# Moving one group of TensorE transposes ahead of a matmul in an attention step

## The chip, the cores and the metric

The kernel runs on one NeuronCore of a Trainium2 chip. The metric is device time in microseconds. Five runs of the kernel before took 1192.12, 1193.80, 1199.54, 1202.81 and 1203.57 us; the median is 1199.54 us. One further run was made with the hardware profiler on; all views of the trace quoted here come from that one.

## The reference

The input x holds 64 sequences of 64 tokens with 512 features, in fp32. Four layers are added to it, each with its own residual, and each takes an index per sequence:

```python
x = x + L0(x, cond)            # per sequence a 64 x 64 matrix out of 200, over the tokens
x = x + L1(x, adapter1)        # 512 x 512 product plus a low-rank adapter, rank 16 of 4
x = x + L2(x, tables, kv_lens) # attention with a paged cache, a window of 256 positions
x = x + L3(x, adapter3)        # 512 x 512 product plus a low-rank adapter, rank 16 of 8
```

The change lies in the attention. For each sequence, 8 query heads share 4 key heads (64 features each). The new keys (normed and rotated) and new values of the 64 tokens are written into blocks of the cache. A token attends to the 256 positions up to its own: `softmax(q @ k.T / 16)` over them, times the values. The cache is reached through a table of blocks, 16 positions a block, of which at most 21 bear on a sequence.

## The kernel before, in words

There are two stages. In the first one (0 to about 460 us) the layers 0 and 1 and the key and value projections run over 32 tiles of 128 tokens. In the second one (from about 476 us on) the attention and layer 3 run, and the change touches that stage alone.

The order of the instructions is written out by hand (`tc.manual_schedule()`): what the program issues first on an engine runs first on it. The framework only adds the waits between engines.

The second stage is a loop over 128 **steps**. A step is one sequence `b` and one pair `gp` of key heads; `q = b // 4` is the **group** of four sequences, so a group has 8 steps, and `i = s % 8` is the **position** of a step in its group. Every step `s` does this, in this order on TensorE:

- `scores(s + 1)` (L983): the products of queries and turned keys of the next step, into the banks `psc` of PSUM;
- `turn_p(s)` (L1025): six transposes of the softmax weights, into the banks `pp`;
- for positions 4 to 7 `k_turn(q + 1, *turn1)`, the **first key turn**;
- one part of layer 3 of the group before (`out_product` L1059, `ranks` L1067, `y_first` L1078, `y_rest` L1084 and L1086), or in the first two groups a query projection (L263);
- `values(s)` (L1041): the turned weights times the values, into the one bank of `psO`;
- for positions 3 to 6 `k_turn(q + 1, *turn2)`, the **second key turn**.

Then the next step's `scores` follow. A key turn (`k_turn`, L175) makes four transposes of 84 x 128 pieces of the next group's keys out of the tile `k` (named `k2` in the code) into the only bank of the pool `psK`, and two copies (L183, L184) take them from there to `kT_mem`, on ScalarE where `o4` is even and on VectorE where it is odd. The eight turns of a group are spread like this:

```python
turns = {3: (None, (0, 0)), 4: ((1, 0), (0, 1)), 5: ((1, 1), (0, 2)), 6: ((1, 2), (0, 3)),
         7: ((1, 3), None)}
```

The pairs are `(gp, o4)`. So the second turn at position 3 is the first of its group, and the one at position 6, `(0, 3)`, is the last for the key heads `gp = 0`; the step at position 7 begins with `scores(s + 1)`, which is the first to read them.

What else bears on the turns: the tile `k` is filled by gathers (`k_load`), copies (`k_copy`, L157) and last by `k_patch(q + 1)` at position 1, an indirect DMA from GpSimd's queue that writes the rows of new keys over the old ones. On VectorE a step has `maxima` (L999), a copy of one turned half (L1032), `shares` (L1016, L1017) and, where `gp` is 1, the middle part of `window` (L972). On ScalarE it has the other copy of L1032, `exponentials` (L1009), the outer parts of `window` (L971, L973), the copy `keep_o` of the values' product (L1049, after the second turn's copies) and, where `gp` is 0, `v_copy` (L197), for which a `v_patch` on GpSimd's queue waits. The last group has no next one, so 15 groups have key turns inside the loop.

Of the kernel before, what the change touches and what calls it, by code (L numbers as in the profile page):

```python
# [50 lines left out]
def kernel(  # L51
# [89 lines left out]
    def bank(pool, name):  # L141
        return pool.tile([P, 512], F32, name=name, tag="b")
# [5 lines left out]
    def k_load(q, h):  # L148

        if q < B // 4:  # L150
            gather(kt[:NP, 2 * h : 2 * h + 2].rearrange("p g o d -> p (g o d)"), k_halves,
                   ik_old[:, h, q : q + 1])
# [8 lines left out]
    def k_patch(q):  # L161

        if q < B // 4:
            gather(k2[:NP].rearrange("p o g d -> p (o g d)"), pk, ik_new[:, q : q + 1], NWR - 1)

    def kT(q, gp):
        return kT_mem[q % 2][:, gp].rearrange("p (b o c i) -> p b o c i", b=4, o=3, c=4)

    def k_turn(q, gp, o4, pool=psK):

        if q >= B // 4:
            return
        ps = bank(pool, f"psk{q}_{gp}_{o4}")[:, : 4 * NP].rearrange("p (o r) -> p o r", o=4)
        for oq in range(4):
            PE.transpose(ps[:, oq, :],  # L175
                         k2[:NP, 4 * oq + o4, 2 * gp : 2 * gp + 2].rearrange("p g d -> p (g d)"),
                         ident[:NP, :NP])
        if o4 < 3:
            dst = kT(q, gp)[:, :, o4, :3]
        else:  # L180
            dst = kT(q, gp)[:, :, :, 3]
        copy = V.tensor_copy if o4 % 2 else S.copy
        copy(dst[:, :, :, :NR], ps[:, :3].rearrange("p c (b j) -> p b c j", b=4))  # L183
        copy(dst[:, :, :, NR:], ps[:, 3].rearrange("p (b c j) -> p b c j", b=4, c=3))  # L184

    def v_load(b):
        if b < B:
            for g in range(NG):
                gather(vs_mem[:NV, b % 2, g].rearrange("p o d -> p (o d)"), v_rows,
                       iv_old[:, b, g : g + 1])  # L190

    def vt(b):
        return vt_mem[:, b % 4].rearrange("p (o g d) -> p o g d", g=NG, d=HD)
# [5 lines left out]
    def v_patch(b):  # L199
        if b < B:  # L200
            gather(vt_mem[:NV, b % 4], pv.rearrange("w (q r) -> (w q) r", q=4),
                   iv_new[:, b : b + 1], NWR * 4 - 1)

    def v_share(b):

        if b < B:
            for c in range(3):
                DMA.dma_start(out=vt(b)[96:NVK, c], in_=vt(b)[32 * c : 32 * c + 28, 3])
# [49 lines left out]
    def product_q(n, pool):  # L258
        if 0 <= n < NTILE:
            psq[n] = bank(pool, f"q{n}")  # L260
            xt = x2s.pop(n)
            for c in range(KC):
                PE.matmul(psq[n], lhsT=xt[:, c, :], rhs=wq_sb[:, c, :],  # L263
                          start=(c == 0), stop=(c == KC - 1))

    def norm_q(n):

        if not 0 <= n < NTILE:
            return lambda: None
        rest = turned(n, psq.pop(n), NH, qsc, "q", qp1, qp2)  # L270

        def second():
            qheads[n] = rest()
        return second

    def turn_q(n, pool):
        if not 0 <= n < NTILE:
            return
        ps = bank(pool, f"pst{n}").rearrange("p (gp h b t) -> p gp h b t", gp=2, h=2, b=2)
        hq = qheads.pop(n).rearrange("p (gp h g) d -> p gp h (g d)", gp=2, h=2)  # L280
        for gp in range(2):
            for h in range(2):
                PE.transpose(ps[:, gp, h].rearrange("p b t -> p (b t)"), hq[:, gp, h], ident)
        qt = qp2.tile([P, 2, 2, 2, T], F32, name=f"qt{n}", tag="qt")
        for gp in range(2):
            S.copy(qt[:, gp].rearrange("p b h t -> p h b t"), ps[:, gp])
        lo = n % 2 * 2
        for gp in range(2):
            S.dma_start(out=qd[:, n // 2, gp, lo : lo + 2], in_=qt[:, gp])
# [668 lines left out]
    def q_load(q):  # L958
        if q < B // 4:
            qts[q] = ap2.tile([P, 2, 4, 2, T], F32, name=f"qs{q}", tag="qs")  # L960
            DMA.dma_start(out=qts[q], in_=qd[:, q])

    def x_load(q):
        xqs[q] = ap2.tile([P, KC, 256], F32, name=f"xq{q}", tag="xq")
        DMA.dma_start(out=xqs[q], in_=x2d[:, :, q * 256 : (q + 1) * 256])
# [9 lines left out]
    def scores(s):  # L975

        if s >= NST:
            return
        q, b, gp = steps[s]
        pscs[s] = [bank(psC, f"psc{s}_{g}")[:, :NS] for g in range(2)]  # L980
        for g in range(2):
            gs = slice(g * HD, (g + 1) * HD)
            PE.matmul(pscs[s][g], lhsT=qts[q][gs, gp, b % 4].rearrange("p h t -> p (h t)"),  # L983
                      rhs=kT(q, gp)[gs, b % 4].rearrange("p o c i -> p (o c i)"),
                      start=True, stop=True)
# [4 lines left out]
    def maxima(s):  # L990

        if s >= NST:
            return
        b = steps[s][1]
        sms[s] = []
        for g in range(2):
            sm = sm_mem[:, (2 * s + g) % 4]
            mn = ap4.tile([P, 1], F32, name=f"mn{s}_{g}", tag="mn")
            V.tensor_tensor_reduce(rows4(sm)[:, :, :, :28], rows4(pscs[s][g]), rows4(pens[b]),  # L999
                                   SCALE, 3.0e38, ALU.add, ALU.min, mn)  # L1000
            rsum = ap4.tile([P, 1], F32, name=f"rsum{s}_{g}", tag="rsum")
            sms[s].append((sm, mn, rsum))

    def exponentials(s):
        if s >= NST:
            return
        for sm, mn, rsum in sms[s]:
            w = rows4(sm)[:, :, :, :28]
            S.activation(w, w, AF.Exp, bias=mn, scale=-1.0, accum_out=rsum)  # L1009
# [9 lines left out]
    def turn_p(s):  # L1019

        pps[s] = []
        for g in range(2):
            pp = bank(psP, f"pp{s}_{g}")[:, : 3 * P].rearrange("p (o r) -> p o r", o=3)
            for o in range(3):
                PE.transpose(pp[:NVK, o, :], sms[s][g][0][:, o * P : o * P + NVK], ident)  # L1025
            pps[s].append(pp)

    def keep_p(s):
        pTs[s] = []
        for g in range(2):  # L1030
            pT = ap2.tile([NVK, 3, P], F32, name=f"pT{s}_{g}", tag="pT")
            (V.tensor_copy if g else S.copy)(pT, pps[s][g][:NVK])  # L1032
            pTs[s].append(pT)

    def values(s):

        q, b, gp = steps[s]
        po = bank(psO, f"po{s}")[:, :P]
        for o in range(3):
            for g in range(2):  # L1040
                PE.matmul(po[g * HD : (g + 1) * HD, :], lhsT=vt(b)[:NVK, o, 2 * gp + g],  # L1041
                          rhs=pTs[s][g][:, o, :], start=(o == 0), stop=(o == 2))
        return po

    def keep_o(s, po):
        q, b, gp = steps[s]
        if s % 8 == 0:
            oTs[q] = ap2.tile([P, 2, 4, 2, T], F32, name=f"oT{q}", tag="oT")
        S.copy(oTs[q][:, gp, b % 4].rearrange("p h t -> p (h t)"), po)  # L1049
# [67 lines left out]
    for s, (q, b, gp) in enumerate(steps):  # L1117
        i = s % 8
        turn1, turn2 = turns.get(i, (None, None))
        if i == 0 and q:  # L1120
            x_load(q)
        if i == 2:
            q_load(q + 1)
        if gp == 0:
            v_load(b + 3)
        else:
            v_share(b + 1)
            v_patch(b + 2)
        if i == 1:
            k_patch(q + 1)  # L1130
        if i in (2, 3):
            k_load(q + 2, i - 2)
        scores(s + 1)
        turn_p(s)
        if 0 < s < 16:
            turn_q(nq + s - 2, psO)
        if turn1:
            k_turn(q + 1, *turn1)
        maxima(s + 1)
        keep_p(s)  # L1140
        exponentials(s + 1)
        second = norm_q(nq + s if q < 2 else -1)
        if parts:
            parts.pop(0)()
        if q < 2:
            product_q(nq + s + 1, psM)
            x2_load(nq + s + 3)
        shares(s + 1)
        second()
        if gp:  # L1150
            window(b + 2)
        po = values(s)
        if turn2:
            k_turn(q + 1, *turn2)
        keep_o(s, po)
        if gp == 0:
            v_copy(b + 2)
        if i == 0:
            k_copy(q + 1, 3)
        elif i > 4:  # L1160
            k_copy(q + 2, i - 5)
        if i == 7:
            parts += last_parts(q)
# [53 lines left out]
```

## Time and profile before

| | |
|---|---|
| median of five runs | 1199.54 us |
| the profiled run, its own time | 1194.86 us |
| its span, first to last instruction | 1193.1 us |
| TensorE matmuls busy | 1097.9 us (92%) |
| VectorE, ScalarE, GpSimd busy | 752.8, 570.8, 615.2 us |
| 700 to 800 us: TensorE, VectorE, ScalarE, GpSimd busy | 95.76, 64.56, 62.50, 63.76 us of 100 |

PE is the matmul part of TensorE, PEld its weight loads, DVE is VectorE, ACT ScalarE, POOL GpSimd, SP the engine that only issues DMAs. A line of a timeline has the start in us, the length in us, engine, line of the code, operation, what is written and read, and in square brackets the time that the engine sat idle before it with what ended the idle time. The fp32 matmuls run as two passes each, so six products of `values` show as x12; the transposes show as x1 each.

### The profile page before, as it was taken

To read this page: it belongs to the slowest core of one execution; us is meant where nothing else is said; L and a number is where in the kernel's file an instruction comes from. 1 tells how busy PE (TensorE), PEld (TensorE's weight loads), DVE (VectorE), ACT (ScalarE), POOL (GpSimd) and SP (SyncE) were. 2 spreads that over 40 slices of the span, in tenths; PEclk is the share of its full clock that TensorE was granted. 3 is DMA by queue.
4 is the path that set the end of the run, shared out by engine and by line. 5 is a ranking of instruction groups with operands and counts; after the bars stand their busy time and mean duration, and the time that the engine had idled before them with its cause. 6 is when DMAs were issued, how large, how long until landed. Compare 5 with 4: busy or idle time off the path is not lost.

```text
span 1193.1 us, 17686 instructions
## 1 busy us (share of the span) xinstructions
PE 1097.9 (92%) x5622; PEld 638.1 (53%) x5622; DVE 752.8 (63%) x2313; ACT 570.8 (48%) x1472; POOL 615.2 (52%) x601
## 2 busy tenths in 40 slices
PE   4998899999899995897999999999999999999998
PEld 4444444444444443455566556656656665665665
DVE  3676445756666593786667666666766676666561
ACT  1332212223224332555566666656666665666561
POOL 3153231333263253588766667667666666756620
PEclk9999999999899997898999999999999999999999
DMA  7266622132433264354565566557556755755420
GB/s 260 108 256 227 228 91 91 61 125 73 156 100 98 85 173 130 105 146 127 133 160 147 141 138 159 133 131 170 144 138 152 168 133 136 164 146 138 99 66 36
DMA packets 129820, 163.20 MB, mean 137 GB/s; under 512 B 58079, under 2 KB 96891, under 8 KB 125545
## 3 DMA queue, kind: packets, MB, share of 16 engines
q0 software_dynamic: 63872, 85.04, 29.3%
q1 hardware_dynamic: 46416, 53.89, 14.9%
q10 hardware_dynamic: 19440, 23.15, 5.7%
q8 instruction: 45, 0.74, 0.3%
q14 instruction: 47, 0.39, 0.1%
HBM read 139.66 MB, written 50.33 MB: 159 GB/s over the span
## 4 chain that ended last, share of the span: by engine, by line
PE 63%; DVE 10%; DMA 9%; ACT 6%; issue 5%; POOL 2%; ACTq 1%; POOLq 0%; DVEq 0%; SPq 0%
PE pso L1059 7%; PE pp L1025 6%; PE po L1041 6%; PE psc L983 6%; PE q L263 6%; PE ps L787 5%; PE kv L820 5%; PE psy L1084 5%; PE psy L1078 5%; DMA k<-pk,ik_new 4%; PE psk L175 3%; PE psxa L1067 2%; PE psy L1086 2%; PE ps L789 2%; PE psz L772 1%
## 5 line engine op out<-in xcount | busy, mean ns | idle before, releaser
L65 POOL DMA_INDIRECT vs_mem<-in_vblk_dram,iv_old x256 | 310.7, 1214 | 77.4 <-issue 65.8
L1009 ACT ACTIVATE sm_mem<-sm_mem,mn 128x336 f32<-128x336 f32 x256 | 145.6, 574 | 32.9 <-DVE mn L999 31.8
L65 POOL DMA_INDIRECT vt_mem<-pv,iv_new x64 | 79.7, 1245 | 130.1 <-ACT vt_mem L197 68.7
L999 DVE CUSTOM_DVE_ANT_0 sm_mem<-psc,pen 128x336 f32<-128x336 f32 x256 | 118.7, 500 | 14.1 <-PE psc L983 12.4
L1041 PEld LDWEIGHTS po<-pT,vt_mem 124*64 124x64 f32 x1536 | 83.2, 137 | 75.1 <-ACT sm_mem L1009 53.1
L1059 PE MATMUL pso<-oT,woT_sb 128*128 128x256 f32 x512 | 123.3, 385 | 0.0
L263 PE MATMUL q<-wq_sb,x2q 128*128 128x512 f32 x256 | 120.5, 616 | 0.0
L983 PE MATMUL psc<-kT_mem,qs 64*128 64x336 f32 x512 | 108.1, 497 | 10.8 <-DVE kT_mem L184 10.8
L1041 PE MATMUL po<-pT,vt_mem 124*64 124x128 f32 x1536 | 114.4, 282 | 3.6 <-ACT pT L1032 3.6
L787 PE MATMUL ps<-kT_mem,kT_mem 128*128 128x512 f32 x256 | 116.9, 600 | 0.6 <-PE ps_fill L493 0.6
L1017 DVE TENSOR_SCALAR sm_mem<-sm_mem,rsum 128x336 f32<-128x336 f32 x256 | 110.8, 433 | 9.1
L820 PE MATMUL kv<-wkv_sb,xr 128*128 128x512 f32 x256 | 115.4, 595 | 0.4 <-ACT va L828 0.4
L1025 PE MATMUL pp<-ident,sm_mem 128*124 128x128 f32 x768 | 113.5, 282 | 2.5 <-DVE sm_mem L1017 1.8
L1025 PEld LDWEIGHTS pp<-ident,sm_mem 128*124 128x124 f32 x768 | 81.1, 139 | 63.6 <-issue 51.5
L248 POOL TENSOR_TENSOR q<-q,rsq 128x512 f32<-128x512 f32 x30 | 32.1, 1074 | 141.1 <-DVE rsq L246 110.4
L1059 PEld LDWEIGHTS pso<-oT,woT_sb 128*128 128x128 f32 x512 | 92.7, 193 | 12.4 <-ACT oT L1049 2.7
L787 PEld LDWEIGHTS ps<-kT_mem,kT_mem 128*128 128x128 f32 x256 | 49.2, 193 | 61.3 <-issue 60.1
L263 PEld LDWEIGHTS q<-wq_sb,x2q 128*128 128x128 f32 x256 | 49.9, 200 | 59.2 <-issue 58.9
L175 PE MATMUL psk<-ident,k 84*128 84x84 f32 x512 | 63.4, 250 | 16.4 <-ACT kT_mem L184 13.7
L820 PEld LDWEIGHTS kv<-wkv_sb,xr 128*128 128x128 f32 x256 | 47.0, 191 | 57.1 <-issue 55.6
L1032 ACT COPY pT<-pp 124x384 f32<-124x384 f32 x128 | 61.7, 482 | 31.3 <-PE pp L1025 25.2
L973 ACT ACTIVATE pen<-pen,edge 128x336 f32<-128x336 f32 x64 | 36.9, 576 | 79.8 <-DVE pen L972 79.8
(223 smaller groups left out, 1783.5 us busy)
## 6 DMA issues: line engine op xcount, KB each, us to landing
xt<-in_x_dram SPq DMA_DIRECT2D x32, 256.0 KB
x2d<-xr SPq DMA_DIRECT2D x8, 1024.0 KB
x2q<-x2d SPq DMA_DIRECT2D x32, 256.0 KB
qd<-qt ACTq DMA_DIRECT2D x64, 128.0 KB
qs<-qd SPq DMA_DIRECT2D x16, 512.0 KB
xq<-x2d SPq DMA_DIRECT2D x16, 512.0 KB
out_dram<-ys ACTq DMA_DIRECT2D x32, 256.0 KB
vt_mem<-vt_mem SPq DMA_DIRECT2D x192, 28.0 KB
```

Source lines behind the costliest of these rows:

```text
L65: G.indirect_dma_start(out=dst, out_offset=None, in_=src, in_offset=bass.IndirectOffsetOnAxis(ap=idx, axis=0), **more,)
L175: PE.transpose(ps[:, oq, :], k2[:NP, 4 * oq + o4, 2 * gp : 2 * gp + 2].rearrange("p g d -> p (g d)"), ident[:NP, :NP])
L263: PE.matmul(psq[n], lhsT=xt[:, c, :], rhs=wq_sb[:, c, :], start=(c == 0), stop=(c == KC - 1))
L787: PE.matmul(ps, lhsT=wb_sb[:, c, oc * P : (oc + 1) * P], rhs=x1_mem[:, c, :], start=(c == 0), stop=False)
L820: PE.matmul(pskv[n], lhsT=xrs[s][:, c, i * P : (i + 1) * P], rhs=wkv_sb[:, c, :], start=(c == 0), stop=(c == KC - 1))
L983: PE.matmul(pscs[s][g], lhsT=qts[q][gs, gp, b % 4].rearrange("p h t -> p (h t)"), rhs=kT(q, gp)[gs, b % 4].rearrange("p o c i -> p (o c i) ...
L999: V.tensor_tensor_reduce(rows4(sm)[:, :, :, :28], rows4(pscs[s][g]), rows4(pens[b]), SCALE, 3.0e38, ALU.add, ALU.min, mn)
L1009: S.activation(w, w, AF.Exp, bias=mn, scale=-1.0, accum_out=rsum)
L1017: V.tensor_scalar(w, w, rsum, None, ALU.mult)
L1025: PE.transpose(pp[:NVK, o, :], sms[s][g][0][:, o * P : o * P + NVK], ident)
L1041: PE.matmul(po[g * HD : (g + 1) * HD, :], lhsT=vt(b)[:NVK, o, 2 * gp + g], rhs=pTs[s][g][:, o, :], start=(o == 0), stop=(o == 2))
L1059: PE.matmul(o, lhsT=woT_sb[:, c, ec * P : (ec + 1) * P], rhs=oT[:, c // 2, :, c % 2, :], start=(c == 0), stop=(c == 3))
```

## The change

The second key turn is issued ahead of `values(s)` in place of after it. Nothing else moves; the copies of the turn still stand ahead of `keep_o` on ScalarE, and in the same place among the others on VectorE.

```diff
         if gp:
             window(b + 2)
-        po = values(s)
         if turn2:
             k_turn(q + 1, *turn2)
+        po = values(s)
         keep_o(s, po)
```

## The prediction

> **What bounds the kernel now.** I read the page's busy shares first, then TensorE's waits over the loop, then the timeline around each second key turn. TensorE is busy for 92% of the span and nearly 97% in a full group of the loop (40.38 of the 41.80 us from 812.00 to 853.80), while no other engine passes 28 us there. So a move inside TensorE's queue is worth what it does to TensorE's few waits. These are they, from 470 to 1160 us (who waited for what: total us, times, longest us):
>
> ```profile
> PE psk L175 <- ACT kT_mem L184: 13.7, 24, 4.0
> PE psc L983 <- DVE kT_mem L184: 10.8, 16, 1.2
> ...
> PE psk L175 <- DMA k<-pk,ik_new: 2.8, 5, 0.8
> ```
>
> Three of them touch the moved turns. The second line is the scores of position 7, which need keys whose turn TensorE issued just before: 14 times 0.66 us (9.3 us) and once 1.17 us. The third is the turn of position 3, which waits for the patch of the keys to land. The first is the first turn of positions 4 and 6, which wait for ScalarE to empty the one bank of `psK`; 4.0 us of its 13.7 lie ahead of the loop.
>
> The other work in the queue is only put in another order: four transposes take 0.44 us from start to the next group's start (838.99 to 839.43), the values' 12 passes 0.81 us (838.18 to 838.99). The change moves 15 x 4 = 60 turns, no copy and no DMA; VectorE's, ScalarE's, GpSimd's and SP's queues keep their order.
>
> **Position 6, the wait that should go.** TensorE first, then VectorE, same microseconds:
>
> ```profile
> 838.18 0.88 PE L1041 MATMUL po<-pT,vt_mem 124*64 124x128 f32 x12
> 838.99 0.51 PE L175 MATMUL psk<-ident,k 84*128 84x84 f32 x4
> 840.16 0.84 PE L983 MATMUL psc<-kT_mem,qs 64*128 64x336 f32 x4 [0.66 <-DVE kT_mem L184]
> ```
>
> ```profile
> 838.76 0.39 DVE L1017 TENSOR_SCALAR sm_mem<-sm_mem,rsum 128x336 f32<-128x336 f32 x1
> 839.54 0.42 DVE L183 COPY kT_mem<-psk 128x252 f32<-128x252 f32 x1 [0.38 <-PE psk L175]
> 839.88 0.23 DVE L184 COPY kT_mem<-psk 128x84 f32<-128x84 f32 x1
> ```
>
> After the move the transposes start at 838.18 and end by 838.69. One would write off the whole wait, but VectorE is not free then: the shares stand ahead of the copies in its queue and end at 839.15. So the copy starts near 839.12 (such neighbours overlap by some hundredths) in place of 839.54, and the scores, which come 0.62 us after the copy's start, at 839.74 in place of 840.16. **Gain 0.42 us**, and a wait of about 0.3 us is left, since TensorE has done turn and values by 839.43. All 14 groups from the second on show the same 0.66 us: 14 x 0.42 = 5.9 us. In the first group VectorE is busy with the queries' norms up to the very copy:
>
> ```profile
> 539.73 0.67 DVE L244 TENSOR_TENSOR q<-q,mq 128x512 f32<-128x512 f32 x1
> 540.33 0.41 DVE L183 COPY kT_mem<-psk 128x252 f32<-128x252 f32 x1
> ```
>
> There the turn ended at 539.77 and the copy waited for VectorE alone, so its 1.17 us stay: gain 0. The bounds of this gain are 0 (all groups like the first) and the whole 10.5 us (9.3 + 1.17).
>
> **Position 3, the wait that should grow.** The turn of position 3 needs the patch, which lands near the values:
>
> ```profile
> 694.79 0.88 PE L1041 MATMUL po<-pT,vt_mem 124*64 124x128 f32 x12
> 696.50 0.51 PE L175 MATMUL psk<-ident,k 84*128 84x84 f32 x4 [0.83 <-DMA k<-pk,ik_new]
> 696.94 0.84 PE L983 MATMUL psc<-kT_mem,qs 64*128 64x336 f32 x4
> ```
>
> ```profile
> 852.89 9.73 DMA k<-pk,ik_new
> 862.62 0.04 issue
> 862.67 0.51 PE psk L175 x4
> ```
>
> Today 0.81 us of values run while the patch is still under way. With the turn ahead, they wait behind it. From the trace's semaphore records I took the landing (the last of the patch's sixteen updates, plus the 0.04 us of the row above) against the start of the values, group by group, in us: -3.24, -0.70, -0.28, 0.62, 1.71, 0.53, 0.75, 0.18, 1.46, 1.14, -0.15, -0.03, 0.57, 1.58, 1.24. A negative one costs nothing. Where it is over 0.81 TensorE waits already (5 groups, the 2.8 us above) and will wait 0.81 longer: **5 x 0.81 = 4.05 us**. The five between 0 and 0.81 are new waits, but part of each is time that the first turn of position 4 loses today anyhow, as ScalarE comes to the copy only behind the window:
>
> ```profile
> 821.99 0.58 ACT L973 ACTIVATE pen<-pen,edge 128x336 f32<-128x336 f32 x1 [2.00 <-DVE pen L972]
> 822.48 0.36 ACT L183 COPY kT_mem<-psk 128x252 f32<-128x252 f32 x1
> ```
>
> ```profile
> 823.01 0.51 PE L175 MATMUL psk<-ident,k 84*128 84x84 f32 x4 [0.30 <-ACT kT_mem L184]
> ```
>
> That copy's time is set by VectorE's part of the window, not by TensorE's turn, so a later turn eats that wait first: 0.62 - 0.30, 0.53 - 0.30, 0.75 - 0.61, nothing of 0.18, 0.57 - 0.24, in all 1.0 us. **Loss at position 3: 5.1 us.** Its bounds are 0 (every patch in time) and 15 x 0.81 = 12.2 us (every patch late).
>
> **Positions 4 and 5, and the rest.** Their scores do not read the turned keys, so nothing is gained. What they could lose is the one bank of `psK`: with values gone from between, the second turn comes 0.81 us sooner after the first one's copies. Those end at 824.05, 830.71 and 837.03 (positions 4, 5, 6), and the second turns would start at 826.93, 832.65 and 838.18: 1.15 us to spare at the least. The Trainium skill, "Perfetto Trace Analysis", section "Matmuls", would have independent groups rotate through different PSUM banks so that one's copies overlap the next one's matmuls; by that rule this change, which brings two turns of one bank closer, is a step backwards, and the sum would be positive. In these rows it costs nothing, since a layer-3 part (1.75 us or more) still stands between the two turns; without that cover one copy pair (0.5 us, 823.55 to 824.05) a turn would show, 45 x 0.5 = 22 us.
>
> The copies of the even turns sit behind the window on ScalarE (822.48 and 835.46, turns done at 821.14 and 833.97), so an earlier turn does not bring them forward, and the 0.45 us at position 6 and 0.30 at position 4 stay. `keep_o` at positions 4 and 6 comes 0.44 us later and pushes `v_copy`, and GpSimd's patch behind it; ScalarE has 0.45 and 1.18 us idle ahead of its next copy there, and GpSimd 4.01 us idle at 840.68 before the next of these patches: 0. Should one of them not be covered, 0.44 us x 30 = 13 us is the end of that scale. The transposes may need a wait instruction of their own for the bank: the nearest row, such an instruction on TensorE's queue, takes 51 ns, and the matmuls ahead hide it; uncovered, 60 x 0.051 = 3 us. Other neighbours in the array could overlap better or worse by the 0.09 us that separates the overlaps seen (0.07 and 0.16 us); at a tenth of that for 60 moves, 0.5 us either way.
>
> **Sum.** -5.9 + 5.1 = **-0.8 us**, against the profiled run's 1194.86 us (span 1193.1 and 1.76 us around it): 1194.1. That run lies 4.7 us below the median; against 1199.54 the same difference gives **1198.7 us**. A difference of some 1% is about what a measurement of this kernel can tell from no change, and this one is far below.
>
> **Rivals.**
> 1. *The patch is late in every group* (slower). Landing after issue ranges from 7.09 to 10.17 us in this one run, so another run can be worse; 10 of 15 groups already land after the values start. Price 0.81 us a group: +12.2 - 5.9 = +6.3, 1205.8 us. It decides for slower as soon as the mean loss passes 5.9 / 15 = 0.39 us a group; it is 0.34 in this run.
> 2. *The patch is in time* (faster): three early groups and two later ones landed before the values. Then only the gain stands, -5.9, 1193.6 us; if in addition VectorE were free when the turn ends, -10.5, 1189.0 us, against which its shares at 838.76 speak.
> 3. *The change does not do what it says*: VectorE, not the turn, sets the scores' start everywhere as it does in the first group, the gain is 0 and the loss stays: +5.1, 1204.6 us. Against it speaks the 0.38 us that VectorE idles for the turn.
>
> **How the numbers follow.** My sum, with the loss between 2.5 and 8 us: 0.58. Rival 1: 0.17. Rival 2: 0.14. Rival 3: 0.06. An uncovered cost of the list above: 0.05. Rivals 1 to 3 differ from the median by less than 1% (12 us), so "within 1%" holds nearly all: 0.92; the 0.04 on each side is for a cover that fails and for the median's own scatter, 1192 to 1204 in the five runs. The range reaches from halfway between rival 2's two times to just past rival 1, 1191 to 1207.
>
> **What would show it.** Right: position 7's scores wait 0.2 to 0.35 us for VectorE in place of 0.66; the turn of position 3 waits for the patch in about ten groups and 6 to 12 us in all, in place of 5 and 2.8; the first turns' waits at position 6 stay 0.45. Wrong: new waits of second turns for ScalarE or VectorE (the bank), values waiting for anything but the turn, or patches that land at another distance from their issue than 7 to 10 us.

## The result, and the profile after

The change makes the kernel slower by 0.5%: 1208.1 us, the median of 42 runs, against 1199.74 us of 79 runs of the kernel before. The ratio of the two is 1.0049 with a 95% interval from 1.0035 to 1.0064; it counts only runs within 1.5% of the fastest of their kernel, which leaves out a quarter of the changed kernel's runs, the profiled one among them, and so lies below the quotient of the medians (1.0070). The forecast was 1198.7 us, its range ended at 1207.

The profiled run took 1212.88 us (span 1211.1 us), 4.8 us more than the median, while the one of before had been 4.9 us faster than its median. So the two traces lie 18 us apart where the medians lie 8.4 us apart: the traces show what the change does, and overstate how much.

Of the page of the kernel after, here are the row of the granted TensorE clock by fortieths of the span, and the row of all key turns (times, mean ns, then idle time ahead of them):

```profile
PEclk9999999999999996998999989999999999999999
...
L175 PE MATMUL psk<-ident,k 84*128 84x84 f32 x512 | 62.0, 248 | 34.3 <-DMA k<-pk,ik_new 19.6
```

The same view as before the change, TensorE's waits (here from 470 to 1180 us; total us, times, longest us):

```profile
PE psk L175 <- DMA k<-pk,ik_new: 19.6, 11, 3.6
PE psk L175 <- ACT kT_mem L184: 14.5, 18, 4.2
PE psc L983 <- DVE kT_mem L184: 6.3, 16, 1.2
```

The third line is the wait that was to shrink, and it did, from 10.8 to 6.3 us. The first is the one that was to grow. It grew from 2.8 to 19.6 us, from 5 groups to 11, and its longest from 0.8 to 3.6 us. This is the timeline of TensorE in the group with a wait of 3.48 us, and under it four windows (TensorE's busy time first, the granted clock in the third column from the end):

```profile
694.20 1.89 PE L1059 MATMUL pso<-oT,woT_sb 128*128 128x256 f32 x8
699.57 0.82 PE L175 MATMUL psk<-ident,k 84*128 84x84 f32 x4 [3.48 <-DMA k<-pk,ik_new]
700.32 1.55 PE L1041 MATMUL po<-pT,vt_mem 124*64 124x128 f32 x12
701.79 1.49 PE L983 MATMUL psc<-kT_mem,qs 64*128 64x336 f32 x4
703.22 1.54 PE L1025 MATMUL pp<-ident,sm_mem 128*124 128x128 f32 x6
```

```profile
694.00:698.00 4.00, 2.09 (x11) 1.53 (x10) 2.82 (x11) 2.00 (x6) 3.08 (x4) 1.00 0.68 146
698.00:702.00 4.00, 2.43 (x18) 1.92 (x20) 0.47 (x1) 1.16 (x4) 2.46 (x3) 0.60 1.08 221
702.00:706.00 4.00, 4.00 (x17) 2.97 (x18) 1.50 (x5) 0.82 (x4) 2.88 (x3) 0.55 0.89 152
706.00:710.00 4.00, 4.00 (x27) 2.63 (x25) 1.93 (x7) 1.35 (x5) 0.00 (x0) 1.00 0.35 73
```

Something follows the wait that my sum did not have: the clock falls to half. The values take 1.55 us where they take 0.88 at the full clock, the scores 1.49 where they take 0.84, and the six transposes 1.54 for 0.87. Against the undisturbed order of the same rows this group loses 2.8 us from the end of its wait of 3.48 us to the end of the half clock. The trace's clock records put the stretch of half clock from 698.81 to 705.63 us, 6.83 us long. There are four of them after 560 us: behind the waits of 3.48 and 3.58 us (6.83 us each) and of 2.48 and 2.29 us (3.41 us each). The waits of 1.62 us and less have none, and the trace of before has none from 560 to 1192 us. A faster run shows the same: in after3 of the third study (1229.72 us on a chip where the kernel before takes 1236) waits of 3.62 and 2.67 us for the patch came with 6.83 and 3.41 us of half clock.

The scores of position 7, TensorE first, then VectorE:

```profile
843.90 0.46 PE L175 MATMUL psk<-ident,k 84*128 84x84 f32 x4
844.28 0.87 PE L1041 MATMUL po<-pT,vt_mem 124*64 124x128 f32 x12
845.50 0.84 PE L983 MATMUL psc<-kT_mem,qs 64*128 64x336 f32 x4 [0.34 <-DVE kT_mem L184]
```

```profile
844.57 0.40 DVE L1017 TENSOR_SCALAR sm_mem<-sm_mem,rsum 128x336 f32<-128x336 f32 x1
844.88 0.41 DVE L183 COPY kT_mem<-psk 128x252 f32<-128x252 f32 x1
845.22 0.23 DVE L184 COPY kT_mem<-psk 128x84 f32<-128x84 f32 x1
```

The copy stands right behind the shares, without idle time, and the scores wait 0.34 us in place of 0.66.

To see where time goes, I took the starts of the `scores` as marks and averaged the length of each position's step over twelve groups (steps 24 to 119). All tables below are made in this way; us:

| position | 0 | 1 | 2 | 3 | 4 | 5 | 6 | 7 | a group |
|---|---|---|---|---|---|---|---|---|---|
| before | 4.26 | 4.10 | 4.11 | 4.87 | 6.96 | 5.72 | 6.26 | 5.28 | 41.56 |
| after | 4.38 | 4.10 | 4.11 | 6.54 | 7.05 | 5.57 | 5.94 | 5.28 | 42.98 |

Positions 5 and 6 gain 0.15 and 0.32 us, position 0 loses 0.12, and position 3 loses 1.67. The whole, 1.42 us x 14 = 19.9 us, is the 18 us between the spans within 2 us.

### The profile page after: what moved, and what is told of

The parts are those of the page before. It is cut to its first block, busy times and chain, and to the rows that moved or that the text cites. A ratio compares the mean times of both kernels' runs of the same rounds, so it can differ in the third digit from the quotient of the medians.

```text
span 1211.1 us, 17728 instructions
## 1 busy us (share of the span) xinstructions
PE 1098.5 (91%) x5622; PEld 647.4 (53%) x5622; DVE 755.6 (62%) x2313; ACT 572.6 (47%) x1472; POOL 616.0 (51%) x601
## 4 chain that ended last, share of the span: by engine, by line
PE 57%; DVE 13%; DMA 11%; ACT 7%; issue 4%; POOL 4%; ACTq 1%; POOLq 0%; DVEq 0%; SPq 0%
DMA k<-pk,ik_new 8%; PE ps L787 7%; PE kv L820 6%; PE pp L1025 6%; PE psc L983 5%; PE po L1041 5%; PE pso L1059 5%; PE q L263 5%; PE psy L1084 5%; PE psk L175 3%; PE psy L1078 3%; PE psxa L1067 2%; PE psy L1086 2%; PE ps L789 2%; DVE sm_mem L1017 2%
## 5 line engine op out<-in xcount | busy, mean ns | idle before, releaser
L1041 PE MATMUL po<-pT,vt_mem 124*64 124x128 f32 x1536 | 117.4, 285 | 3.4 <-ACT pT L1032 3.4
L1017 DVE TENSOR_SCALAR sm_mem<-sm_mem,rsum 128x336 f32<-128x336 f32 x256 | 114.5, 447 | 9.1
L1025 PE MATMUL pp<-ident,sm_mem 128*124 128x128 f32 x768 | 116.1, 287 | 2.7 <-DVE rsum L1016 1.6
L983 PE MATMUL psc<-kT_mem,qs 64*128 64x336 f32 x512 | 111.1, 510 | 6.3 <-DVE kT_mem L184 6.3
L175 PE MATMUL psk<-ident,k 84*128 84x84 f32 x512 | 62.0, 248 | 34.3 <-DMA k<-pk,ik_new 19.6
L175 PEld LDWEIGHTS psk<-ident,k 84*128 84x128 f32 x512 | 52.7, 147 | 68.0 <-DMA k<-pk,ik_new 24.5
```

What stands on the lines that cost most here:

```text
L175: PE.transpose(ps[:, oq, :], k2[:NP, 4 * oq + o4, 2 * gp : 2 * gp + 2].rearrange("p g d -> p (g d)"), ident[:NP, :NP])
L1017: V.tensor_scalar(w, w, rsum, None, ALU.mult)
```

## The experiments

**Theory A** at the outset: the loss is the turn of position 3, which waits for the key patch, with the lower clock behind long waits; positions 4 to 6 carry the gain. **Theory B**: `v_copy`, which comes later at positions 4 and 6 (behind `keep_o`), pushes GpSimd's gathers and so the patch or a `v_patch`; then positions 4 to 6 carry the loss.

**First study: the change in parts, and `v_copy` first.** The parts differ in one condition (`i == 3`, `i != 3`, `i == 6`):

```diff
-        if turn2:
+        if turn2 and i == 3:
             k_turn(q + 1, *turn2)
         po = values(s)
+        if turn2 and not (i == 3):
+            k_turn(q + 1, *turn2)
```

`after_vfirst` is the whole change and this:

```diff
         po = values(s)
+        if i in (4, 6):
+            v_copy(b + 2)
         keep_o(s, po)
-        if gp == 0:
+        if i in (0, 2):
             v_copy(b + 2)
```

The turn ahead at position 3 alone:

> The second turn stands ahead of the values at position 3 alone; positions 4, 5 and 6 are as before. Theory A (the patch: the turn of position 3 waits for the patch's landing, a longer wait also lowers the granted clock, and positions 4 to 6 gain about 0.6 us a group): this part alone is slower than the whole change, some +8 to +18 us (ratio 1.007 to 1.015), waits of the turn for the patch of 10 to 20 us in all, and the patch lands 8.9 us after its issue as before. Theory B (the queue: the moves at positions 4 and 6 push the copy of the cached values, and with it GpSimd's gathers, closer to the patch, so that it lands 0.7 us later): without those moves the landing is back at 8.9 us and the loss is that of the forecast, +5 us (1.004). Theory C (the bank of the turns at positions 4 to 6 costs the time): +0 to +5 us here.

At positions 4, 5 and 6 alone:

> The second turn stands ahead of the values at positions 4, 5 and 6; at position 3 it stays behind them. Theory A: the gain alone, 14 groups of 0.62 us, -8.7 us, so about 1191 us (0.993); waits for the patch near the 2.8 us of before; no drop of the granted clock after 560 us. Theory B: the patch lands 0.7 us later here too (9.6 us after issue), the waits for it grow to 6 to 10 us, and the gain shrinks to -2 to -5 us (0.996 to 0.998). Theory C: slower than before, with waits of turns at positions 4 to 6 for their bank.

At position 6 alone:

> Only the second turn of position 6 stands ahead of the values. Theory A: the scores of position 7 wait 0.3 us in place of 0.66, -5 to -6 us (0.995 to 0.996), as the forecast had it; the further 0.15 us a move come from a turn that follows a layer-3 product and not the values, so positions 4 and 5 are missing here and the gain is 2 to 4 us less than in the run with 4, 5 and 6. Theory B: the patch lands later by 0.5 us or more, since the copy of the cached values at position 6 is the last one that gathers wait for ahead of the patch; gain 0 to -3 us.

With `v_copy` first:

> The whole change, and at positions 4 and 6 the copy of the cached values stands ahead of the copy of the values' product on ScalarE, so that it need not wait for the values and GpSimd's gathers start about 1 us earlier. Theory A: the landing of the patch does not depend on it; the time stays at that of the whole change, +5 to +8 us (1.004 to 1.007), with waits for the patch of 15 to 20 us. Theory B: the landing comes back to 8.9 us or less after the issue, the waits for the patch fall to 6 to 10 us, no or few drops of the clock, and the time falls to -2 to +2 us.

Measured, as a ratio to the kernel before: p3_only 0.9974 (0.9934 to 1.0014), p456 0.9982 (0.9944 to 1.0019), p6_only 0.9930 (0.9885 to 0.9975), after_vfirst 0.9942 (0.9906 to 0.9978). No part is slower, though Theory A expected a loss of p3_only, and the whole with `v_copy` first is faster. But the kernel before took 1234.98 us here, not 1200. Each study ran on one chip, another one each time; I call this a difference of chips, though no chip was met in two studies, so that something else that differs between the studies isn't ruled out. What follows is only that the first comparison may not hold here, so the change itself had to run on such a chip.

**Second study: the unaltered change, its parts again, and an earlier patch.** `after2` is the changed kernel. `after_early` is the changed kernel with the patch and the copy that it waits for one place earlier in their queues:

```diff
         else:
             v_share(b + 1)
+            if i == 1:
+                k_patch(q + 1)
             v_patch(b + 2)
-        if i == 1:
-            k_patch(q + 1)
...
+        if i == 0:
+            k_copy(q + 1, 3)
         if gp == 0:
             v_copy(b + 2)
-        if i == 0:
-            k_copy(q + 1, 3)
-        elif i > 4:
+        if i > 4:
             k_copy(q + 2, i - 5)
```

The unaltered change:

> The changed kernel again, unaltered, beside its parts on one chip. If the chip is like the one of the first comparison (the patch lands about 9 us after its issue, the kernel before takes about 1200 us): ratio 1.003 to 1.007, 15 to 20 us of waits for the patch. If it is like the one of the first four experiments (kernel before about 1235 us, patch landing 11 us or more after its issue): 0.994 to 1.000, since there the turn waits for the patch in either order and the moved order costs only what the values would have covered.

Positions 4, 5 and 6:

> Second turn ahead of the values at positions 4, 5 and 6 alone, on this chip. Theory A (position 3 alone loses): 0.992 to 0.995 against before, and 6 to 15 us faster than the whole change. Theory B (later gathers make the patch land later): 0.996 to 1.000, landing 0.5 us or more later than in the kernel before on a like chip.

Position 3:

> Second turn ahead of the values at position 3 alone, on this chip. Theory A: slower than the whole change by what positions 4 to 6 gain (6 to 9 us), so 1.008 to 1.013 on a chip like the first. Theory B: +5 us or less (1.000 to 1.004), with the landing 8.9 us after the issue and no drop of the clock.

The earlier patch:

> The whole change, with the patch issued earlier: at position 0 the copy that the patch waits for stands ahead of the copy of the cached values on ScalarE, and at position 1 the patch stands ahead of the other patch in GpSimd's queue, so that it is issued some 1.8 us earlier in the step. Theory A: the turn's waits for the patch fall from about 20 us to 4 us or less, the clock no longer drops, and the gain of positions 4 to 6 shows: 0.993 to 0.996 on a chip like the first. If the loss sat in anything else of the move than the patch's landing, the time stays at that of the whole change (1.003 to 1.007).

Measured, with the kernel before at 1243.5 us: after2 0.9896 (0.9837 to 0.9955), p456_2 0.9931 (0.9889 to 0.9972), p3_only_2 0.9924 (0.9887 to 0.9961), after_early 0.9882 (0.9845 to 0.9919). The unaltered change is faster here by 1.0%, the other way round than in the first comparison, and bringing the patch forward adds nothing that these intervals tell apart.

**Third study: is that sign real?** `before2` is a copy of the kernel before, to see whether a kernel that differs in nothing is measured as equal.

The copy of the kernel before:

> The kernel before, unaltered, run as if it were a variant. It tells two things: the profile of the kernel before on this chip, and whether a mere copy differs from it. Expected: 0.999 to 1.001. If the copy comes out below 0.997, then the gains of all variants on the chips where the kernel before takes 1235 to 1243 us hold a part that has nothing to do with the order of the turns.

The unaltered change:

> The changed kernel, unaltered, beside the kernel before on one chip, for the waits by position. On a chip where the kernel before takes about 1200 us: 1.003 to 1.007, turns of position 3 waiting 15 to 20 us for the patch. On one where it takes about 1240 us: 0.988 to 0.996.

Positions 4, 5 and 6:

> Second turn ahead of the values at positions 4, 5 and 6 alone. Theory A (the loss sits at position 3): on a chip with the kernel before at about 1200 us 0.992 to 0.995; on one with 1240 us 0.993 to 0.998. Theory B (later gathers make the patch land later): 0.996 to 1.000 on the first kind.

Position 3:

> Second turn ahead of the values at position 3 alone. Theory A: 1.008 to 1.013 on a chip with the kernel before at about 1200 us, by the wait for the patch and the clock that drops after the long ones; on one with 1240 us between 0.992 and 1.002. Theory B: 1.000 to 1.004 on the first kind, without drops of the clock.

Measured, with the kernel before at 1236.06 us: before2 1.0005 (0.9954 to 1.0055), after3 0.9951 (0.9914 to 0.9989), p456_3 0.9963 (0.9926 to 1.0001), p3_only_3 0.9996 (0.9955 to 1.0036). A copy is equal, and the change is again faster. The profiles show where, though the two lie only 5.5 us apart where the medians lie 10.7 apart. The steps on this chip:

| position | 0 | 1 | 2 | 3 | 4 | 5 | 6 | 7 | a group |
|---|---|---|---|---|---|---|---|---|---|
| before2 | 4.25 | 4.10 | 4.11 | 6.25 | 8.04 | 5.72 | 6.28 | 5.28 | 44.05 |
| after3 | 4.38 | 4.10 | 4.15 | 6.44 | 7.91 | 5.57 | 5.94 | 5.28 | 43.79 |

The kernel before is longer by 1.38 us at position 3 and by 1.08 us at position 4 than in the first trace, and nowhere else: 2.49 us a group, 35 us in 14 groups, of the 40 us between the two spans. The change does to positions 0, 5 and 6 what it did there, but adds only 0.19 us at position 3. TensorE's waits from 470 to 1200 us of before2, then of after3:

```profile
PE psc L983 <- DVE kT_mem L184: 11.1, 16, 1.2
PE psk L175 <- issue: 8.3, 17, 1.2
PE po L1041 <- ACT pT L1032: 8.0, 7, 1.6
PE psk L175 <- ACT kT_mem L184: 7.4, 6, 3.2
PE po L1041 <- issue: 6.6, 14, 1.1
```

```profile
PE psk L175 <- ACT kT_mem L184: 18.8, 22, 3.3
PE psk L175 <- DMA k<-pk,ik_new: 8.6, 5, 3.6
...
PE psc L983 <- DVE kT_mem L184: 5.1, 15, 0.3
...
PE po L1041 <- ACT pT L1032: 3.3, 3, 1.6
...
PE po L1041 <- issue: 1.5, 5, 0.5
```

On this chip the values themselves wait, 14.6 us in all (8.0 + 6.6), because the turned weights reach them late. The turn ahead stands in that gap: the values' waits fall to 4.8 us, and this 9.8 us pays for the new waits of the turn. Those are only in part under the patch's name: between 560 and 1150 us the traces of these chips hold 58 to 65% of the DMA landings, the four of 1200 us 96 to 98%, so a wait under `issue` may have lost its cause here. With all names together the turn of position 3 waits 3.9 us in the twelve groups of before2 and 13.2 us in those of after3, 9.4 us more. At position 3 alone the values' wait falls from 0.67 to 0.05 us a group. So the turn has cover here that it does not have where the kernel before takes 1200 us.

What makes the values wait shows on ScalarE. Its timeline at position 2 in before2, and in the trace of before:

```profile
839.64 0.19 ACT L1009 ACTIVATION_READ_ACCUMULATOR sm_mem<-sm_mem,mn 128x1 f32 x1
842.96 0.27 ACT L1049 COPY oT<-po 128x128 f32<-128x128 f32 x1 [3.12 <-PE pp L1025]
```

```profile
815.73 0.19 ACT L1009 ACTIVATION_READ_ACCUMULATOR sm_mem<-sm_mem,mn 128x1 f32 x1
816.64 0.27 ACT L1049 COPY oT<-po 128x128 f32<-128x128 f32 x1 [0.71 <-PE po L1041]
```

`keep_o` copies the values' product, which in before2 starts at 839.62 and lasts 0.88 us. It is done at 840.5, and the copy comes at 842.96. The median over twelve groups is 2.1 us from the product's end to the copy's start, against 0.05 us in the trace of before, and VectorE takes up the scores of positions 3 and 4 later too (1.38 and 1.15 us for 0.03). At the other positions both traces have the same distances. So TensorE's results of positions 2 to 4 are taken up late on these chips.

**Fourth study: the patch without the wait.** The patch keeps its gather and its bytes but writes a tile that nobody reads, in the kernel before and in the changed one:

```diff
+    spare = mp.tile([P, 4096], F32, name="spare")
+    G.memset(spare, 0.0)
...
-        if i == 1:
-            k_patch(q + 1)
+        if i == 1 and q + 1 < B // 4:
+            gather(spare[:NP], pk, ik_new[:, q + 1 : q + 2], NWR - 1)
```

The kernel before, so edited:

> The kernel before, with the patch of the keys written into a spare tile: the same gather and the same bytes, but the new keys of groups 1 to 15 never reach the scores (this part of the computation is left out), and no turn waits for the patch. Theory A (the wait for the patch at position 3 makes the change's loss): against the kernel before -2.8 us, the five waits that its profile shows, on a chip where the kernel before takes about 1200 us; up to some 20 us less where it takes 1235 us and position 3 is 1.4 us a group longer, if that length is a wait for the patch, and nothing if it is not. Theory B (the patch has no part in it): no difference beyond 0.3%.

The changed kernel, so edited:

> The changed kernel with the same edit: the patch goes to a spare tile, the new keys of groups 1 to 15 are left out of the scores, and no turn waits for the patch. Theory A: faster than before_elsewhere by the gain of positions 5 and 6 less the loss of position 0, 14 x (0.15 + 0.32 - 0.12) = 4.9 us, 0.4%, on any chip, and on a chip of 1200 us faster than the unaltered change by some 12 us or more; no wait of a turn of position 3 for a DMA in its profile and no halved clock behind one. Theory B: it stands to before_elsewhere as the change stands to the kernel before on a 1200 us chip, slower by 0.5%.

The two parts of the change once more, with the patch in its place:

> The turn ahead of the values at position 3 alone. Theory A: on a chip where the kernel before takes about 1200 us slower than before by 0.6 to 1.0% (the waits for the patch of the changed kernel's profile, 19.6 us less the 2.8 us of before, less what position 4 gets back); on one where it takes 1235 us within 0.3% of before, as in the three runs so far. Theory B: within 0.3% on both.

> The turn ahead of the values at positions 4, 5 and 6 alone. Theory A: on any chip faster than before by 14 x (0.15 + 0.32 - 0.12) = 4.9 us, 0.4%. Theory B (these positions carry the loss on a 1200 us chip): slower there by 0.5%.

Measured, with the kernel before at 1235.06 us: before_elsewhere 1242.89 us, 1.0067 (1.0038 to 1.0096); after_elsewhere 1225.03 us, 0.9927 (0.9889 to 0.9965); p3_only_4 0.9953 (0.9924 to 0.9982); p456_4 0.9946 (0.9916 to 0.9977). Neither theory foresaw the first: without any wait for the patch the kernel before is not faster but 0.7% slower, and `keep_o` of position 2 still comes 2.1 us late. So the extra length of positions 3 and 4 on these chips is not a wait for the patch. Between the two kernels without the wait the change gains 1.4% (0.9856 by the medians, 0.981 to 0.992 by drawing again from the 9 and 12 runs), more than the 0.5 to 1.0% with it, which agrees with Theory A in sign, though the interval overlaps that of after2, and is more than the 0.4% that Theory A expected. Of the two parts, p3_only_4 has 8.8 us of waits for the patch in 6 groups in its profile, and p456_4, whose turn at position 3 stays behind the values, 3.9 us of waits of that turn in all, the longest 1.8 us.

**Fifth study: no patch.** The two lines are left out:

```diff
-        if i == 1:
-            k_patch(q + 1)
```

The kernel before, then the changed one:

> The kernel before without the patch of the keys in its loop: the new keys of groups 1 to 15 are left out of the scores, and the gather with its 16 KB packets is gone. Theory D (the patch's transfer makes the hand-offs of positions 2 to 4 late on a chip where the kernel before takes 1235 us): keep_o of position 2 starts 0.05 us after its product again, positions 3 and 4 shorten by 2.5 us a group, some 35 us, to about 1200 us. Theory E (another transfer or the chip itself does it): the hand-offs stay 2.1 us late and the time within 0.7% of before. On a chip of 1200 us both expect no more than the five waits for the patch, 2.8 us.

> The changed kernel with the same edit, the new keys of groups 1 to 15 left out. Theory D: there is neither a wait for the patch nor a late hand-off, so only the gain of positions 5 and 6 less the loss of position 0 is left, 14 x (0.15 + 0.32 - 0.12) = 4.9 us, 0.4% faster than before_nopatch, about 1195 us on either kind of chip. Theory E: on a chip of 1235 us it stands to before_nopatch as after_elsewhere to before_elsewhere, 1.4% faster, near 1225 us.

This one ran where the kernel before takes 1200.51 us, as in the first comparison. Measured: before_nopatch 1189.65 us, 0.9903 (0.9866 to 0.9940); after_nopatch 1183.53 us, 0.9862 (0.9821 to 0.9903). Against each other, the change is faster by 6.1 us, 0.5% (0.9949 by the medians; 0.991 to 0.9997 by drawing again from the six runs of each), where in the first comparison, with the patch, it is slower by 0.5%; the two intervals do not meet. The changed kernel with its patch was not run in this study, so this rests on the kernel before taking 1200 us in both. Take the patch away and the sign turns: **the loss is the patch**. Where the time goes, the positions show (us):

| position | 0 | 1 | 2 | 3 | 4 | 5 | 6 | 7 | a group |
|---|---|---|---|---|---|---|---|---|---|
| before_nopatch | 4.26 | 4.10 | 4.11 | 4.55 | 7.02 | 5.72 | 6.27 | 5.28 | 41.30 |
| after_nopatch | 4.39 | 4.10 | 4.11 | 4.40 | 7.04 | 5.57 | 5.95 | 5.28 | 40.84 |

0.46 us a group, 14 groups: 6.4 us, against 6.1 measured. TensorE's waits of after_nopatch from 470 to 1150 us, and its clock row:

```profile
PE psk L175 <- ACT kT_mem L184: 17.8, 29, 3.9
...
PE psc L983 <- DVE kT_mem L184: 5.1, 15, 0.3
```

```profile
PEclk9999999999899998898999999999999999999999
```

No turn waits for a DMA, and the clock records have no half clock from 558 to 1181 us. Position 3 of the changed kernel is 2.14 us shorter than with the patch (4.40 for 6.54), that of the kernel before 0.32 us (4.55 for 4.87). The patch's traffic is gone along with the wait, but in the fourth study the traffic stayed, only the wait went, and the change gained too.

One expectation missed here. The kernel before was to gain 2.8 us from losing its five waits, and gained 10.9. Its profiled run (span 1192.8 us) does not show them: it was the slowest of its six, as the profiled run of before was among the fastest of its own. That the patch costs a usual run of the kernel before more than that one trace shows would explain it, and so would the transfer itself, which is gone together with the wait; neither is shown. Whether the patch's transfer makes the late hand-offs of the other chips, this study cannot say, since it ran on a chip that has none.

## Why the prediction was wrong

**What bounds the kernel** held: TensorE, and the sign was decided by its waits.

**The gain at position 6** held. Predicted were 0.42 us a group and a wait of about 0.3 us left; the wait left is 0.34 us, and positions 5 and 6 together are 0.47 to 0.49 us shorter on both kinds of chip. It is split otherwise than I put it: position 5 gives 0.15 us, since a turn behind a layer-3 product and ahead of the values overlaps a little better than behind the values, and position 6 gets 0.32: the wait falls by 0.32 and the overlap gives the same 0.15, but its first turn now waits 0.60 us for ScalarE where I had it stay at 0.45. Position 0 gives 0.12 us back in its values' passes, which I did not look for. Without the patch the whole is 6.1 us; the sum had 5.9. That these agree so closely is luck, since smaller terms of both signs that the sum did not have make up for the 0.42 that was not reached.

**The first group** held: a wait of 1.2 us is left in it. **Positions 4 and 5 and the one bank of `psK`** held as well: no second turn waits for ScalarE or VectorE in after_nopatch, so the cover of a layer-3 part was there. What I priced at 0 on GpSimd was misread. The 4.01 us that GpSimd sits idle ahead of the `v_patch` are no cover, since the copy `v_copy` itself ends them:

```profile
840.68 1.23 POOL L65 DMA_INDIRECT vt_mem<-pv,iv_new  x1 [4.01 <-ACT vt_mem L197]
```

In the trace of after this `v_patch` is indeed issued 0.44 us later in its step, and the gathers behind it with it. What that costs comes below.

**The loss at position 3** is the step that failed. The mechanism was the one I gave: the turn waits for the patch in 11 groups ("about ten"). The size was not. I took the landing of each patch from one profiled run as a fixed time, let each late group lose at most the 0.81 us of the values, and so had 9.5 us of waits in all (2.8 + 4.05 + the five new ones, 2.65) and a net loss of 5.1. Two things are wrong with that:

- *The landing does not stand still.* From issue to landing the patches took 8.87 us on average in the trace of before and 9.60 in that of after, 10.6 to 12.0 in the four groups with the long waits. In 12 of the 15 groups the patch is issued 3.2 us after the scores that open position 1, in both traces, and the turn could start 8.3 to 8.6 us after that in both, so the lateness lies in the transfer alone. Those 0.73 us more, in 14 groups, are 10.2 us, about the distance between 9.5 and 19.6. The values had been slack for such a patch, and a wait only adds: an early patch gives nothing back. What I called the upper bound, 12.2 us for 15 late patches, bounds only the cover that is removed, not the transfers that come later still. I had named landings outside 7 to 10 us as a sign of being wrong, and 5 of the 15 are. Whether they come later through the change or from run to run stays open in the main. With the turn of position 6 moved, the last gather ahead of the patch is issued 5.56 us before it in place of 6.20 (medians), which is Theory B's path. On the chips of 1235 us the patch's last 16 KB packet ends 8.39 us after the issue in the eight runs with that move and 8.23 in the six whose gathers stay at 6.20, with ranges that overlap (8.20 to 8.47, 8.07 to 8.38); between the traces of before and after it is 8.00 and 8.58. So at most a part of the 0.6 us looks like the change's own.
- *The clock.* Waits of 2.29 us and more were followed by 20.5 us of half clock in all, which costs at most half of that, 10.2 us. No wait of position 3 in the trace of before was longer than 0.83 us, so nothing in it showed this price, and I had none for it.

In the traces the account closes: 16.8 us more of waits for the patch (19.6 - 2.8), 8.4 to 10.2 for the clock (2.8 us for a stretch of 6.83 us as in the group shown, or half of all 20.5), less 4.9 for positions 0, 5 and 6, less 2.2 for the first turn of position 4, whose wait of 0.22 us a group went down to 0.06: 18.1 to 19.9 us, where the positions have 19.9 and the spans 18.0. By the medians, 8.4 us of loss and 6.1 us of gain leave 14.5 us for the loss at position 3, in place of 5.1; by the ratio of 1.0049, 5.9 and 6.1 leave 12.0.

**The rivals.** Rival 1 (the patch late in every group) had the right place and side. Its price, 12.2 us, is at the low end of the 12.0 to 14.5 above, but not by its own account: 11 of 15 groups waited, and some for 3.58 us with a fallen clock behind it, where it had 0.81 us in each. Rival 2 is what the run without the patch shows: 6.1 us gained, for the 5.9 it names. Rival 3 fell: the gain is there in every trace. The range had rival 1 as its upper end, which made that end a sum over one run's landings.

**The Trainium skill**, "TensorE: Matmul & The Clock Gate", Part 1, bears on the failed step and had been left out: it describes a monitor that halves TensorE's clock after an idle window of about 3.4 us, which runs freely and does not start with the idle time. The runs agree in the two clocks and in the length of the slow stretches (3.41 and 6.83 us). They differ in how much idle time it takes: a wait of 2.29 us was enough in this trace, and less in others (last section).

What is left open: how much of the patch's later landing is the change's doing, why TensorE's results are taken up late on the chips of 1235 us, and how the turn ahead at positions 4 to 6 alone does where the kernel before takes 1200 us. On the other chips that part was measured at 0.9982, 0.9931, 0.9963 and 0.9946 in four studies; on a chip of 1200 us it did not run.

## What to carry to other kernels

Before you move a transfer's consumer ahead of other work, count that work as slack for the transfer, and price its removal by the spread of landing times over several runs, not by the landings of one trace; lateness adds up and earliness is lost. Ask of every wait that brings TensorE more than about 1.4 us of idle time in 3.4 us what the granted clock does after it. And where two chips of the same type differ by 3%, compare the steps by position before you trust a sign measured on one of them.

## What the runs showed of the hardware

- In the trace of after, waits of TensorE of 2.29 and 2.48 us were followed by 3.41 us at half clock, and waits of 3.48 and 3.58 us by 6.83 us; waits of 1.62 us and less by none. At half clock the values' twelve passes took 1.55 us for 0.88.
- In each of the twenty traces the stretches of half clock begin on one grid of 3.413 us, to within 3 ns. Between 565 and 1150 us, by the traces' records, the clock fell at the end of 54 windows of that grid, and each of them had at least 1.43 us of TensorE idle time. Every window at full clock with more than 1.76 us was followed by half clock and none with less than 1.43 us; of the 39 in between, 20 were. So what counted was the idle time in one window, not the length of one wait.
- The kernel before took 1200 us in the first comparison and in one of the five studies, and 1235 to 1243 us in the other four, each on a chip of its own. The difference sits in two of eight positions, where ScalarE and VectorE take up TensorE's results up to 4 us late (the median for `keep_o` of position 2 is 2.1 us, against 0.05), and the same change is slower by 0.5% in the first comparison and faster by 0.5 to 1.0% on two chips of the other kind. In before2 the lateness begins while the patch, issued at 835.41 us, is under way; its packets of 16 KB are the largest that the gathers move in that stretch. Sending the patch elsewhere did not remove it, and the runs without the patch met a chip without it, so the cause is not known.
